# A four-layer graph network on one core: edges sorted by a scatter and gathered row by row, against edges ranked into tiles of one source and one destination group and fetched by one-hot products

## The chip, the core and the metric

The kernel runs on one core of a Trainium2 chip. The metric is the device time of one execution in microseconds (us), the median of several timed runs. Traces come from a separate, profiled execution of the same program.

## The reference

A graph of N = 12500 nodes with 64 features and E = 200000 edges (src, dst, a type out of 33, a weight) passes through four layers, each added to its input and layer-normalised. The list is sorted by dst.

```python
x = layernorm(x + L0(x))   # two hops on a hyperbolic ball
x = layernorm(x + L1(x))   # two rounds of messages and a GRU cell
x = layernorm(x + L2(x))   # two mean convolutions, 16 hidden
x = layernorm(x + L3(x))   # two mean convolutions, 128 hidden

# L0, per hop: an edge (head = src, tail = dst, relation) makes a message
res = relu(logmap(project(mobius_add(expmap(e[tail], h), expmap(rel, h))), h) + 1e-7 * ricci)
e   = l2_normalize(segment_sum(res, head) / clip(count, 1))    # h = expmap0(e[head])
# L1, per round: linear messages, summed by src, then a GRU
# L2, L3, twice each: segment_sum(x[src], dst) / degree, then two matrices
```

All of L0's maps are vectors times scalars per edge: with dot products of head, tail and relation rows, a chain of scalar operations gives three coefficients per edge, and the message is relu(c0 head + c1 tail + c2 relation). L1 needs per node the sum of x[dst] over its edges by src; L2 and L3 need the sum of x[src] by dst.

## The kernel before

P = 128 partitions. Nodes lie in NB = 98 blocks of 128. The function `fast` does the work; `general` (line 76) is a slower path that runs after it only if a flag says that the edges did not fit the fast path's tiles. Sums in f32 are kept by splitting a table into three bf16 parts (`split`, line 978), multiplying each part by an exact 0/1 matrix, and adding.

1. **Sort (lines 850-960).** VectorE (DVE) and ScalarE (ACT) count edges per source block, a scan gives each edge its slot, and GpSimd (POOL) scatters each column of 128 edges into `meta` in DRAM with one indirect DMA (line 955, 1563 of them). Each source block gets C = 18 columns of 128 edge slots: 98 x 18 = 1764 tiles.
2. **Hops (`hyper_nodes` 1040, `hyper_hop` 1243), twice.** Work goes in 42 steps of HT = 42 tiles, each cut into three of 14. For a tile: POOL gathers the tail rows by an indirect DMA (line 1273, one per tile); SyncE's (SP) queue loads the tile's source and relation indices replicated over the partitions; DVE compares them with the partition number into 0/1 matrices (1291); TensorE (PE) fetches head and relation rows by these (1299, 1303); ACT copies them out of PSUM (1305, 1306). `dots` (1311) multiplies and reduces, `edge_coefficients` (1095) is the chain of 91 small DVE operations with five ACT functions between them, `weigh` (1321) multiplies each row by its coefficient on ACT (1326), `send` (1328) adds the three rows, applies relu and sums by source with an f32 one-hot product (1334, 1337, 1338, 1350). The order on PE, DVE, ACT and POOL is written out by hand (`manual_schedule`) at the end of `hyper_hop`; elsewhere the framework orders the instructions by priority as their buffers come free.
3. **Layer end (1418-1431), then bucketing (1434-1515).** In 7 rounds of 14 source blocks `meta` is read again and each edge is ranked within its pair of source block and group of 512 destinations (NG = 25); `lane` one-hots (1491) times `v` (1470) put the local indices into 98 x 25 = 2450 tiles. Columns `slc`, `dlc` and rows `sl_rows`, `dl_rows` hold them.
4. **Passes.** `sum_to_sources` (1527, twice for L1) and `sum_to_destinations` (1579, four times: two 16 wide, two 64 wide) run over the 2450 tiles. A pass fetches with one 0/1 matrix, ACT casts the result to bf16 (1569, 1620), and a second 0/1 matrix scatters it. The 512-node side takes four matmuls, the 128-node side one: five a tile, of 192 columns (three bf16 parts of 64) or 48.
5. Dense layers (GRU, matrices) follow on blocks of 4 x 128 nodes; they are the same in both kernels.

Of the kernel before, what the change touches and what calls it, by code (L numbers as in the profile page):

```python
# [11 lines left out]
F32 = mybir.dt.float32  # L12
BF16 = mybir.dt.bfloat16
# [40 lines left out]
C = 18  # L54
BCAP = C * P
NTS = NB * C
EC = -(-E // P)
EL = E - (P - 1) * EC
SG = 4 * P
NG = -(-N // SG)  # L60
NBX = 4 * NG
IB = 14
IG = 5
HT = 42
HS_ = 14
HG = 7
TW = D + 3
RW = D + 5
HN = D + 8
SCAN = (163, 300, 550, 550)  # L70
assert sum(SCAN) == EC and IB * C % HT == 0 and HT % HS_ == 0 and HS_ % HG == 0 and NB % IB == 0 and NG % IG == 0

# [722 lines left out]
@with_exitstack  # L795
def tile_gnn_stack(ctx: ExitStack, tc: tile.TileContext, ins, out: bass.AP):
    fl = ctx.enter_context(tc.tile_pool(name="flag", bufs=1))
    flag = fl.tile([1, 1], I32, name="flag")
    fast(tc, ins, out, flag)
    full = tc.nc.values_load(flag[0:1, 0:1], min_val=0, max_val=P)  # L800
    with tc.If(full > 0):
        general(tc, ins, out)
# [3 lines left out]
def fast(ctx: ExitStack, tc: tile.TileContext, ins, out: bass.AP, flag):  # L806
# [12 lines left out]
    def iota(name, shape, pattern, base=0, mult=0, dtype=F32):  # L819
# [4 lines left out]
    iota_n = iota("iota_n", [P, P], [[1, P]])  # L824
    iota_d = iota("iota_d", [P, SG], [[1, SG]], dtype=F16)
    iota_1 = iota("iota_1", [P, P], [[1, P]], base=1, dtype=F16)
    iota_p = iota("iota_p", [P, 4], [[P, 4]], mult=1)
# [4 lines left out]
    before = const.tile([P, P], F32, name="before")  # L832
    pool.affine_select(out=before, in_=ones, compare_op=OP.is_gt, fill=0.0, base=0,
                       pattern=[[1, P]], channel_multiplier=-1)
    viol = const.tile([P, 2], F32, name="viol")

    def weights(name, shape):
        t = const.tile(shape, F32, name=f"w_{name}")
        nc.sync.dma_start(out=t, in_=ins[name])
        return t  # L840

    msg_e = const.tile([P, 2, D], F32, name="msg_e")
    nc.sync.dma_start(out=msg_e, in_=ins["msg_e"].rearrange("t k f -> k t f"))
    msg_n = const.tile([XW, 2, D], F32, name="msg_n")
    nc.sync.dma_start(out=msg_n, in_=ins["msg_n"].rearrange("t k f -> k t f"))
    gru_i = const.tile([D + 1, 2, 3 * D], F32, name="gru_i")
    nc.sync.dma_start(out=gru_i, in_=ins["gru_i"].rearrange("t k f -> k t f"))
    gru_h = const.tile([XW, 2, 3 * D], F32, name="gru_h")
    nc.sync.dma_start(out=gru_h, in_=ins["gru_h"].rearrange("t k f -> k t f"))
    s1_w = weights("s1", [XW, 32])  # L850
    s2_w = weights("s2", [33, D])
    t1_l = weights("t1_l", [D, P])
    t1_r = weights("t1_r", [XW, P])
    t2_w = weights("t2", [P, 2 * D])
    t2_b = const.tile([P, D], F32, name="t2_b")
    nc.sync.dma_start(out=t2_b, in_=ins["t2_b"].to_broadcast([P, D]))

    meta = dram.tile([P * NTS + P * EC, 4], F32, name="meta")  # L860
    meta_v = meta[: P * NTS, :].rearrange("(p v) f -> p v f", p=P)
    with ExitStack() as st:
        sp = st.enter_context(tc.tile_pool(name="sort", bufs=1))
        sw = st.enter_context(tc.tile_pool(name="sort_w", bufs=2))
        spp = st.enter_context(tc.tile_pool(name="sort_p", bufs=1, space=PSUM))

        keys = {}
        for k in ("src", "dst", "etype", "eweight"):
            t = keys[k] = sp.tile([P, EC], F32 if k == "eweight" else I32, name=f"k_{k}")
            vec.memset(t[96:P, EL:], float(P * (P - 1)) if k == "src" else 0.0)  # L870
            flat = ins[k].rearrange("p j -> (p j)")
            rows_in = flat[: (P - 1) * EC].rearrange("(p j) -> p j", j=EC)
            nc.sync.dma_start(out=t[:112, :], in_=rows_in[:112, :])
            nc.sync.dma_start(out=t[112 : P - 1, :], in_=rows_in[112:, :])
            nc.sync.dma_start(out=t[P - 1 : P, :EL], in_=flat[(P - 1) * EC :].unsqueeze(0))

        VQ = NTS // 4
        pad = sp.tile([P, VQ, 4], F32, name="pad")
        vec.memset(pad, 0.0)
        vec.memset(pad[:, :, 0], float(SG * 32))  # L880
        vec.memset(pad[:, :, 1], -1.0)
        for j in range(4):
            nc.sync.dma_start(out=meta_v[:, j * VQ : (j + 1) * VQ, :], in_=pad)

        ib = sw.tile([P, EC], I32, name="ib")
        ts(ib, keys["src"], 7, None, OP.logical_shift_right)
        kb = sp.tile([P, EC], BF16, name="kb")
        copy(kb, ib)


        QB = 42
        edge = sp.tile([P, NB + 1], F32, name="edge")
        pool.iota(edge, pattern=[[-1, NB + 1]], base=0, channel_multiplier=0, allow_small_or_imprecise_dtypes=True)
        ts(edge, edge, 0.5, None, OP.add)
        cnt = sp.tile([P, NB], F32, name="cnt")
        sgn = sp.tile([P, NB + 1], F32, name="sgn")
        for b in range(NB + 1):
            if b < QB:
                junk = sw.tile([P, EC], BF16, name="junk")
                ts(junk, kb, float(b), None, OP.is_equal, OP.add, accum_out=cnt[:, b : b + 1])  # L900
            else:
                junk = sw.tile([P, EC], BF16, name="junk_a")
                act.activation(junk, kb, AF.Sign, bias=edge[:, b : b + 1], accum_out=sgn[:, b : b + 1])
        tt(cnt[:, QB:], sgn[:, QB:NB], sgn[:, QB + 1 :], OP.subtract)
        ts(cnt[:, QB:], cnt[:, QB:], 0.5, None, OP.mult)
        pre = spp.tile([P, NB], F32, name="pre")
        pe.matmul(pre, before, cnt, start=True, stop=True)
        tot = spp.tile([P, NB], F32, name="tot")
        pe.matmul(tot, ones, cnt, start=True, stop=True)
        vec.tensor_reduce(viol[:, 0:1], tot, AX.X, OP.max)  # L910
        first = sp.tile([P, NB], F32, name="first")
        pool.iota(first, pattern=[[BCAP, NB]], base=-1, channel_multiplier=0, allow_small_or_imprecise_dtypes=True)
        tt(first, first, pre, OP.add)

        M = sp.tile([P, EC, 4], F32, name="M")
        copy(M[:, :, 0], keys["dst"])
        ib = sw.tile([P, EC], I32, name="ib")
        ts(ib, keys["src"], P - 1, None, OP.bitwise_and)
        copy(M[:, :, 1], ib)
        act.copy(M[:, :, 2], keys["etype"])  # L920
        act.copy(M[:, :, 3], keys["eweight"])

        n_max = max(SCAN)
        ones_e = sp.tile([P, n_max], BF16, name="ones_e")
        vec.memset(ones_e, 1.0)
        j0 = 0
        for n in SCAN:

            js = slice(j0, j0 + n)
            slot = sw.tile([P, n_max], F32, name="slot")[:, :n]  # L930
            vec.memset(slot, 2.0 * P * NTS)
            for b in range(NB):
                m = sw.tile([P, n_max], I16, name="m")[:, :n]
                ts(m, kb[:, js], float(b), None, OP.is_equal)
                run = sw.tile([P, n_max], F32, name="run")[:, :n]
                vec.tensor_tensor_scan(run, ones_e[:, :n], m, first[:, b : b + 1], OP.mult, OP.add)
                vec.copy_predicated(slot, m, run)
                if j0 + n < EC:
                    act.copy(first[:, b : b + 1], run[:, n - 1 : n])
            over = sw.tile([P, n_max], F32, name="over")[:, :n]  # L940
            stt(over, kb[:, js], -float(BCAP), slot, OP.mult, OP.add)
            none = sw.tile([P, n_max], I16, name="none")[:, :n]
            ts(none, over, float(BCAP), None, OP.is_ge)
            behind = sw.tile([P, n_max], I32, name="behind")[:, :n]
            pool.iota(behind, pattern=[[1, n]], base=P * NTS + j0, channel_multiplier=EC)
            si = sw.tile([P, n_max], I32, name="si")[:, :n]
            copy(si, slot)
            lane = sw.tile([P, n_max], I32, name="lane")[:, :n]
            ts(lane, si, P - 1, None, OP.bitwise_and)
            ts(si, si, 7, None, OP.logical_shift_right)  # L950
            pos = sp.tile([P, n], I32, name=f"pos{j0}")
            stt(pos, lane, float(NTS), si, OP.mult, OP.add)
            vec.copy_predicated(pos, none, behind)
            for c in range(n):
                s = pool.indirect_dma_start(  # L955
                    out=meta[:, :], out_offset=bass.IndirectOffsetOnAxis(ap=pos[:, c : c + 1], axis=0),
                    in_=M[:, j0 + c, :], in_offset=None)
# [875 lines left out]
```

## Time and profile before

| | us |
|---|---|
| timed runs, median of 3 | 16375.89 (16375.42 to 16382.63) |
| profiled execution | 19517.08 |
| its span | 19515.4 |
| sort and scatter | 0 to 2409 |
| hop 1, hop 2 | 2550 to 6905, 7075 to 11425 |
| bucketing | 11660 to 12460 |
| passes of L1 (64 wide) | the first 12480 to 13570, the second up to 15004 |
| passes of L2 (16 wide) | 15436 to 16245, 16250 to 17064 |
| passes of L3 (64 wide) | 17164 to 18300, 18400 to 19450 |

The profiled execution is 3141 us longer than the median. Busy time over the span: PE 9427.2 us (48%), weight loads 8637.0 (44%), DVE 12080.7 (62%), ACT 7308.8 (37%), POOL 5227.6 (27%). The mean granted TensorE clock is 0.694. Lines below are read so: a group gives line, engine, operation, out<-in with shape, count, then busy time, mean ns of one, and idle time before it with what ended it; a timeline row gives start, length, engine, line, count.

### The profile page before, as it was taken

To read this page: it belongs to the slowest core of one execution; us is meant where nothing else is said; L and a number is where in the kernel's file an instruction comes from. 1 tells how busy PE (TensorE), PEld (TensorE's weight loads), DVE (VectorE), ACT (ScalarE), POOL (GpSimd) and SP (SyncE) were. 2 spreads that over 40 slices of the span, in tenths; PEclk is the share of its full clock that TensorE was granted. 3 is DMA by queue.
4 is the path that set the end of the run, shared out by engine and by line. 5 is a ranking of instruction groups with operands and counts; after the bars stand their busy time and mean duration, and the time that the engine had idled before them with its cause. 6 is when DMAs were issued, how large, how long until landed. Compare 5 with 4: busy or idle time off the path is not lost. (4 is left out here: it accounts for less than half of the span.)

```text
span 19515.4 us, 307194 instructions
## 1 busy us (share of the span) xinstructions
PE 9427.2 (48%) x106965; PEld 8637.0 (44%) x106965; DVE 12080.7 (62%) x34976; ACT 7308.8 (37%) x22359; POOL 5227.6 (27%) x5108
## 2 busy tenths in 40 slices
PE   0000013333333313333233323599899888889998
PEld 0000013323232312223222222598798677789898
DVE  6800035555555545554555579997697599988788
ACT  2000024444444424444444430254354233355555
POOL 3877733444344324434433400000000000000000
PEclk9999965555555555555555555798798555589999
DMA  0000031111121131111111110121121133222122
GB/s 16 1 2 2 11 66 44 45 42 46 44 47 44 38 54 45 41 44 47 42 44 43 43 35 6 40 76 57 40 76 54 40 102 101 96 68 75 57 73 72
DMA packets 557119, 934.39 MB, mean 48 GB/s; under 512 B 313712, under 2 KB 316027, under 8 KB 555562
## 3 DMA queue, kind: packets, MB, share of 16 engines
q1 hardware_dynamic: 392650, 790.07, 12.8%
q0 software_dynamic: 162912, 124.55, 4.2%
q8 instruction: 856, 14.02, 0.3%
q14 instruction: 701, 5.74, 0.1%
HBM read 878.49 MB, written 35.70 MB: 47 GB/s over the span
## 5 line engine op out<-in xcount | busy, mean ns | idle before, releaser
L1273 POOL DMA_INDIRECT T<-tab_h,ix x3528 | 3538.0, 1003 | 5367.0 <-DVE HS L1337 3761.4
L1350 PE MATMUL ps<-msg,oh 128*128 128x66 f32 (+1 forms) x7056 | 1549.3, 410 | 3781.3 <-ACT RS L1326 1319.0
L1598 PE MATMUL ps<-gb,d 128*128 128x192 bf16 (+2 forms) x39200 | 3298.1, 232 | 20.3 <-DVE d L1596 12.3
L1350 PEld LDWEIGHTS ps<-msg,oh 128*128 128x128 f32 x7056 | 1503.7, 323 | 3786.0 <-ACT RS L1326 1498.6
L1596 DVE TENSOR_SCALAR d<-iota_d,dl 128x512 bf16<-128x512 f16 x9800 | 2928.4, 349 | 291.2 <-PE ps L1598 45.4
L1598 PEld LDWEIGHTS <-d 128*128 128x128 bf16 x39200 | 2691.9, 107 | 197.8 <-DVE d L1596 30.7
L1620 ACT CAST gb<-pg 128x384 bf16<-128x384 f32 (+2 forms) x4900 | 1692.2, 361 | 1978.1 <-PE pg L1616 1666.8
L1564 PE MATMUL pg<-xs,dt 128*128 128x192 bf16 x19600 | 2049.0, 248 | 168.3 <-DVE dt L1559 168.3
L955 POOL DMA_INDIRECT meta<-M,pos x1563 | 1685.6, 1078 | 717.1 <-issue 475.8
L1299 PE MATMUL ph<-hx,st 128*128 128x69 bf16 x10584 | 767.0, 226 | 2259.5 <-issue 1682.0
L1564 PEld LDWEIGHTS <-dt 128*128 128x128 bf16 x19600 | 1676.7, 99 | 180.2 <-issue 170.9
L1299 PEld LDWEIGHTS <-st 128*128 128x128 bf16 x10584 | 606.4, 119 | 2420.3 <-issue 2088.1
L1569 ACT CAST gb<-pg 128x384 bf16<-128x384 f32 x2450 | 1171.4, 478 | 970.2 <-PE pg L1564 852.9
L1334 DVE TENSOR_TENSOR oh<-iota_n,mt 128x1792 f32<-128x1792 f32 x252 | 508.7, 2019 | 1590.1 <-remote 1328.2
L1616 PE MATMUL pg<-xs,st 128*128 128x192 bf16 (+2 forms) x9800 | 1200.0, 231 | 305.9 <-DVE st L1612 260.8
L1559 DVE TENSOR_SCALAR dt<-row,iota_p 128x640 bf16<-128x640 f16 x3920 | 1225.3, 379 | 71.9 <-PE pg L1564 62.8
L1326 ACT ACTIVATE HS<-HS,wh 128x64 f32<-128x64 f32 x3528 | 1178.3, 334 | 1.5 <-DVE wh L1236 1.5
L1326 ACT ACTIVATE T<-T,wtr 128x64 f32<-128x64 f32 x3528 | 1177.2, 334 | 0.1
L1326 ACT ACTIVATE RS<-RS,wtr 128x64 f32<-128x64 f32 x3528 | 1177.3, 334 | 0.0
L1024 PE MATMUL tr<-ident,mt 128*126 128x128 f32 x28 | 10.2, 459 | 2316.7 <-DMA rel<-in_rel_dram 2299.6
L1352 ACT COPY sums<-ps 128x66 f32<-128x66 f32 (+1 forms) x196 | 41.7, 213 | 2721.7 <-remote 1984.1
L1024 PEld LDWEIGHTS tr<-ident,mt 128*126 128x126 f32 x28 | 5.2, 195 | 2321.7 <-issue 2299.8
(389 smaller groups left out, 15713.7 us busy)
## 6 DMA issues: line engine op xcount, KB each, us to landing
row<-sl_rows SPq DMA_DIRECT2D x700, 448.0 KB
row<-dl_rows SPq DMA_DIRECT2D x196, 800.0 KB
row_st<-s_rows SPq DMA_DIRECT2D x252, 448.0 KB
row_rt<-y_rows SPq DMA_DIRECT2D x252, 448.0 KB
T<-tab_h,ix POOLq DMA_INDIRECT x3528
meta<-M,pos POOLq DMA_INDIRECT x1563
mt<-meta SPq DMA_DIRECT2D x21, 504.0 KB
heads<-hx SPq DMA_DIRECT2D x14, 724.5 KB
```

The lines of the kernel that those rows point to most:

```text
L955: s = pool.indirect_dma_start(out=meta[:, :], out_offset=bass.IndirectOffsetOnAxis(ap=pos[:, c : c + 1], axis=0), in_=M[:, j0 + c, :], in_ ...
L1273: pool.indirect_dma_start(out=T[j][:, k, :], out_offset=None, in_=table[:, :], in_offset=bass.IndirectOffsetOnAxis(ap=edges_of(v)[1][:, v ...
L1299: pe.matmul(ph[:, k, :], hot[0][:, g0 + k, :], edges_of(v)[2][:, v // C % IB, q * RW : (q + 1) * RW], start=q == 0, stop=q == 2)
L1326: act.mul(x, x, c[:, t0 + k : t0 + k + 1])
L1350: pe.matmul(acc["ps"], oh[:, k, :], msg[:, k, :], start=c == 0, stop=c == C - 1)
L1559: ts(dt[:, q, :, :], row[:, g0 : g0 + IG, :], iota_p[:, q : q + 1], None, OP.is_equal)
L1564: pe.matmul(pg[:, len(jobs), :], dt[:, q, g - g0, :], xs[:, 4 * g + q, :], start=q == 0, stop=q == 3)
L1569: act.copy(gb, pg)
L1596: ts(d, iota_d, dl[:, k, b : b + 1], None, OP.is_equal)
L1598: pe.matmul(pss[h // 2][:, h % 2, :], d[:, h * P : (h + 1) * P], gb[:, q, :], start=b == 0 and h % 2 == 0, stop=b == NB - 1, skip_group_ch ...
L1616: pe.matmul(pg[:, len(jobs), :], s[:, b - b0, :], xs[:, b, 0:wx], start=True, stop=True)
L1620: act.copy(gb, pg)
```

## The change

1. **List.** The sort, the scatter and the bucketing go. Both node sides are now cut into NG = 49 groups of GN = 256, which gives 49 x 49 = 2401 pairs, one tile of 128 lanes for each. The list is sorted by dst, so a destination group is one stretch of it. A code 64 * (dst >> 8) + (src >> 8) and six bf16 payload columns (local src, local dst, type, weight in three parts) are written to DRAM in list order; every eighth edge is counted to estimate where each destination group begins.
2. **Windows.** For each of the 49 destination groups a window of 36 x 128 = 4608 edges is loaded. A one-hot `og` of the source group, PE products that count earlier edges of the same pair, and a max tree give each edge its rank; 36 products of `lane` and `v` place the payload in the tiles.
3. **Hops.** A step is one source group, cut into NS = 7 sub-steps of HG = 7 tiles. Tails are fetched like heads, by one-hot products on a table in SBUF (`tabx`, filled by a second `split` in `hyper_nodes`). The sum by source is done in bf16 with the message split in three. The copies into `nn` and `hc` are POOL's. `edge_coefficients` yields after each operation, so that its operations alternate with the bulk of the same sub-step; phases end at "wait".
4. **Passes.** One `sum_pass` for both directions: each side takes two matmuls a tile, four in all. The scattering matrix `s` is one comparison for seven tiles, with the tile index innermost, so that PE reads its columns 14 bytes apart. ACT casts up to 7 tiles together when they are narrow, two at 64 wide.
5. **Other.** The flag tells of a pair with more than 128 edges or an edge outside its window. The loads of the dense layers' weights move from the start to the end of the hops.

The core of the diff:

```python
# list
gd = dst >> 8;  gh = gd[:, ::8]                          # 125 x 1600, 125 x 200
for b in range(NG):
    ts(junk, gh, float(b), None, OP.is_lt, OP.add, accum_out=cnt[:, b : b + 1])
...
for b in range(NG):                                      # windows
    at = nc.sync.value_load(begin[0:1, b : b + 1], ...)
    nc.sync.dma_start(out=code, in_=l_code[ds(at, WIN)]...)
    nc.sync.dma_start(out=pay, in_=l_pay[:, ds(at, WIN)]...)
    ts(ga, code, -64.0 * b, None, OP.add)
    tt(og, iota_a, ga.unsqueeze(1).to_broadcast([P, GA, WC]), OP.is_equal)      # 52 x 36
    for c in range(WC):
        pe.matmul(pc, unit[:, WC-1-c : 2*WC-1-c], og[:, :, c], ...)
    act.copy(per, pc)
    for h in range(WC // RC):
        pe.matmul(prv[:, h], upto, og[:, :, h*RC : (h+1)*RC].rearrange("p a c -> p c a"), ...)
        for c in range(RC):
            pe.matmul(prv[:, h, c, :], later[:, h*RC + c, :], per, ...)
    tt(m, og, prv, OP.mult)
    while n > 1:                                         # 52 -> 26 -> 13 -> 7 -> 4 -> 2 -> 1
        tt(m[:, 0:k, :], m[:, 0:k, :], m[:, n-k : n, :], OP.max)
    ...
    tt(lane, iota_l, rank.unsqueeze(1).to_broadcast([P, P, WC]), OP.is_equal)
    for f in range(NPAY):
        tt(v[:, f], og[:, 0:NG, :], pay[:, f, :].unsqueeze(1).to_broadcast([P, NG, WC]), OP.mult)
    for c in range(WC):
        pe.matmul(po, lane[:, :, c], v[:, :, :, c], start=c == 0, stop=c == WC - 1)
    ...
# hops
def front(n):
    nc.sync.dma_start(out=row, in_=hop_rows[...].to_broadcast([P, HG * 3 * P]))
    ts(o0, row, iota_p[:, 0:1], None, OP.is_equal)               # HG x 3 x 128
    ts(o1, row[:, :, 0:2, :], iota_p[:, 1:2], None, OP.is_equal)
    # per tile: 6 matmuls to ph (head), 6 to pt (tail, from tabx), 3 to pr (relation)
def dots(n):
    pool.tensor_copy(nn[:, 0, s, :], T[n][:, :, 0:3])
    pool.tensor_copy(nn[:, 1, s, :], RS[n][:, :, 0:3])
    pool.tensor_copy(hc[:, s, :], HS[n][:, :, D:])
    for o, x, y in (...):                                        # three times
        tt(q, x, y, OP.mult); yield
        vec.tensor_reduce(o, q, AX.X, OP.add); yield
def part2(n):
    tt(mx[n][:, :, 2*D : 3*D], HS[n][:, :, 0:D], mx[n][:, :, D : 2*D], OP.subtract); yield
    tt(oh, iota_r, slc[:, k, s].unsqueeze(1).to_broadcast([P, GN, HG]), OP.is_equal); yield
    for t in range(HG):
        for q in range(2):
            pe.matmul(ps[k][:, q, :], oh[:, q*P : (q+1)*P, t], mx[n][:, t, :], ...)
PLAN = ((0,), (1,), (2,), (3, 4))       # phases of the coefficients in sub-steps 0 to 3
for s in range(n_all + lag_w + 5):      # lag_w = 13
    banks = front(s)
    weigh(s - lag_w)
    evacuate(s, *banks)                 # three ACT copies
    bulk = chain(part2(s-lag_w-3), add(s-lag_w-1), rest(s-lag_w-2), dots(s-2), ...)
    for _ in chain(*(phase(k) for _ in PLAN[g])):
        next(bulk, None)                # one of the chain, then one of the bulk
    for _ in bulk: pass
    part1(s - lag_w - 2); part0(s - lag_w - 1)
# passes, per group k of IG = 7, per j0 of 7 tiles
for q in range(2):
    ts(o[:, q, :, :], row[:, j0 : j0 + HG, :], iota_p[:, q : q + 1], None, OP.is_equal)
tt(s, iota_r, sc[:, k, j0 : j0 + HG].unsqueeze(1).to_broadcast([P, GN, HG]), OP.is_equal)
for j in range(j0, j0 + HG):
    for q in range(2):
        pe.matmul(pg[:, len(jobs), :], o[:, q, j - j0, :], xs[:, 2*j + q, 0:wx], ...)
    # after an ACT cast to gb, two more:
    #   pe.matmul(ps[:, h, :], s[:, h*P : (h+1)*P, j % HG], gb[:, q, :], ...)
```

`add` is two sums of the three rows, `rest` takes the first bf16 part off the relu'd message, `part0` and `part1` are ACT's casts to the first two parts. In `edge_coefficients` the five ACT functions stand where they stood: tanh ends phase 0, square root phases 1 and 2, two logarithms phase 3.

## Prediction

> **What bounds the kernel now.** I read the windows by stage first. Columns: window, length, then busy time and count for PE, PEld, DVE, ACT, POOL, granted clock, DMA share, GB/s.
>
> ```profile
> 0.00:2409.00 2409.00, 1.15 (x4) 0.93 (x4) 737.00 (x1315) 153.02 (x411) 1689.62 (x1580) 1.00 0.03 4
> 2550.00:6780.00 4230.00, 1319.56 (x13608) 1222.04 (x13608) 2186.49 (x5222) 1816.54 (x6354) 1763.91 (x1764) 0.54 0.19 45
> 11660.00:12460.00 800.00, 287.05 (x1968) 185.81 (x1968) 732.02 (x2128) 60.12 (x257) 0.00 (x0) 0.50 0.02 6
> 15436.00:16245.00 809.00, 705.19 (x12250) 594.30 (x12250) 771.73 (x2659) 272.34 (x1276) 0.00 (x0) 0.53 0.30 102
> 17164.00:18300.00 1136.00, 1079.34 (x12438) 1049.27 (x12438) 928.72 (x2689) 619.57 (x1311) 0.00 (x0) 0.97 0.22 72
> ```
>
> The sort and its scatter are POOL's (2409 us). In a hop no engine is busy over 52%. Bucketing is DVE's. A 16-wide pass is DVE's (772 of 809), a 64-wide one PE's (1079 of 1136). The waits say what holds a hop:
>
> ```profile
> POOL T L1273 <- DVE HS L1337: 3761.4, 121, 91.4
> DVE oh L1334 <- remote: 1328.2, 67, 24.4
> ```
>
> POOL's gathers and DVE wait for each other in a ring. Then rates, from groups and timeline:
>
> ```profile
> L1318 DVE TENSOR_TENSOR q<-HS,T 128x896 f32<-128x896 f32 x252 | 274.8, 1090 | 196.4 <-ACT HS L1305 140.5 <-issue 54.9
> L1479 DVE TENSOR_TENSOR inc<-inc,og x7: 3440/3441/3441, 11658.1 to 12378.5; 128x6300 f16<-128x6300 f16 x7
> L1470 DVE TENSOR_TENSOR v<-og,pay x196: 937/945/960, 11606.1 to 12356.7; 128x450 f16<-128x450 f16 x196
> L1477 PE MATMUL base<-inc,before_h x7: 781/781/781, 11650.6 to 12370.9; 128*128 128x350 f16 x7
> 6779.91 0.33 ACT L1326 ACTIVATE HS<-HS,wh 128x64 f32<-128x64 f32 x1
> 6780.15 0.33 ACT L1326 ACTIVATE T<-T,wtr 128x64 f32<-128x64 f32 x1
> 5018.22 1.43 PE L1299 MATMUL ph<-hx,st 128*128 128x69 bf16 x21
> 5019.46 1.21 PE L1303 MATMUL pr<-relx,rt 128*128 128x67 bf16 x21
> 5020.51 0.85 PE L1299 MATMUL ph<-hx,st 128*128 128x69 bf16 x21
> 5021.20 0.84 PE L1303 MATMUL pr<-relx,rt 128*128 128x67 bf16 x21
> 17331.01 0.82 PE L1598 MATMUL ps<-gb,d 128*128 128x192 bf16 x8
> 17331.67 0.33 PE L1616 MATMUL pg<-xs,st 128*128 128x192 bf16 x2
> 17331.83 0.41 PE L1598 MATMUL ps<-gb,d 128*128 128x192 bf16 x3
> ```
>
> The reader is to see: DVE takes 1.04 ns an element plus 155 in f32, half per element with 16-bit operands in rows (L1479), 1.75 ns when it reads 16-bit elements 36 bytes apart (L1470). A wide strided moving read on PE (L1477) is also slow: I put it at 1.7 ns a column, estimated as the 781 ns less the 180 that L1492's 217 ns for 50 columns leaves beside its columns at 0.8. ACT's weighing muls start 0.24 us apart though 0.33 long. PE's 21 matmuls take 1.24 us in a slow stretch (59 ns each) and 0.69 in a fast one (33). The 192-column pass issues 10 in 0.82 us: 82.5 ns each, weight loads hidden.
>
> **What the Trainium skill says.** "VectorE: DVE Perf Modes", the perf-mode tier table, gives tensor_tensor on 16-bit SBUF operands twice the f32 rate; L1479 agrees (3441 ns against 6717 for L1478 with a PSUM operand). "SBUF — State Buffer", Specifications (TRN2), has 16-byte lines and a penalty for crossing to a new one; L1470 agrees. "TensorE: Matmul & The Clock Gate", Weight-path perf modes, has 128-column 16-bit weights loaded as four parallel chunks "packed or strided"; no run here shows a strided one. "SBUF — State Buffer", Who interferes with whom: a GpSimd op that reads SBUF and a DVE op with two SBUF inputs exclude each other; the trace has no such POOL op.
>
> **Profiled against timed.** The profiled execution took 19517 us, 2 outside its span of 19515; the median is 16376. The missing 3141 I put on the gathers. Outside the two hops (2550-6905 and 7075-11425, 8705 us) lie 10810, so timed hops take 5566, 2783 each, still above DVE's busy 2186 there. PE at 82.5 ns for 192 columns and DVE at its rates have nothing to give, so it can't be spread over the passes. The changed kernel has no gathers, so I take its timed run equal to its profiled one and compare with 16376. Against 19517 the same sum is a fall of 2687, which would be the profile's doing.
>
> **Front end (steps 1, 2).** Removed: sort and scatter 2409, bucketing 800. Added: list arithmetic, 49 counts of 200 elements (0.35 us each, from L900's fixed part), some 12 ops of 1600 elements, loads and stores of the list: 100. Then 49 windows. DVE each: og 1.1, m from PSUM 2.1 (3.4 if its strided PSUM read costs as L1470), six max steps 1.9, lane 2.6, six v of 1764 at 1.07 less overlap 6.0, small ones 1.3: 15-17 us. PE each: 36 po matmuls of 294 columns read 72 bytes apart, 36 x 294 x 1.7 = 18.0; pc 36 x 52 x 1.7 = 3.2; pr 4 x 468 x 1.7 = 3.2; 36 small at 64 ns 2.3; transposes 1: 28. PE works on the next window while DVE ranks this one (two buffers of og, lane and v), so PE's 28 sets the pace; latency and single buffers of pc and pr add 2, my allowance: 30, so 1470, and 20 at the end. Unknown is the strided read at the fast clock: below, 17 us (DVE) a window, 830; above, 41 us if PE and DVE alternate (m to v, 13, beside PE's 28), 2010. The window loads (SP) and rank tables' stores lie beside 210 us of work for 7 windows; uncovered they cost about 5 us a window. Sum 1590. Only inputs with over 128 edges in a pair or outside a window run the general path as well; counted on the reference's inputs, the fullest pair has 118.
>
> **Hops (step 3).** Tiles rise from 1764 to 2401. A sub-step has 7. DVE: o0 2688 elements at L1612's rate (1792 in 680 ns) 0.84, o1 0.65, six dots ops of 448 at 0.65 (467 + 155 + 30 between dependent ones) 3.9, add 1.2, rest 0.65, third part 0.55, oh 1792 16-bit elements 1.05: 8.84, seven times 61.9. Coefficients: 91 ops, 21.0 us by the groups of L1110-L1240, 24 with 49 columns and gaps of 0.035. finish 0.6. Interleaving saves about 0.2 us for each of 34 pairs, 6.8. 79.7 us a group.
> ACT: 21 muls x 0.24 = 5.0, three evacuations 1.4, two parts 1.0, coefficients and three table loads 0.8: 8.3 a sub-step, beneath DVE's 11.4. PE: 105 matmuls at 33-59 ns 3.4-6.2, 14 of 192 columns 1.2-2.3: below too. Rows of 688 KB a sub-step are 60 GB/s, against 102 in the pass above: hidden.
> **New wait:** phases 3 and 4 share a sub-step. DVE's next op after the logarithms waits for ACT, which first evacuates what PE is still multiplying: o0/o1 1.5, PE to about 6.5, evacuation 7.1, table 8.4, two Ln 8.9; DVE arrives at 4.2. It stands 4.8 us once a group, with the rest of dots queued behind it; the next fronts wait for those. Bounds: nothing if ACT runs ahead, 7 with slow PE. A gain is excluded: phase 4 can't start before phase 3 in the same queue.
> 84.5 x 49 = 4140, ramps 60: 4200, both 8400. POOL's three or four small copies a sub-step can each hold DVE up for some 0.2 us, where reduces don't cover them: I take 0.36 us x 686 = 250 (0 to 600). Sum 8650, against 5566 timed: 3084 more. The part of oh that each scattering matmul loads as weights is read 14 bytes apart; even at 220 ns (see the passes) 14 of them bring PE to 3.4-6.2 + 3.1, still below DVE: nothing.
>
> **Passes (step 4).** 2401 tiles x 4 matmuls at 82.5 = 792 (before 12250, 1011), loop ends 98: 890, four times 3560. DVE makes 7 tiles in 1.75 us (two of 896 at 0.37, one of 1792 at 1.01), 250 ns a tile against PE's 330: hidden. 16-wide: DVE's 250 x 2401 = 600 and 100: 700, twice 1400. Sum 4960; before 5999, a gain of 1039. Unknown: s is read 14 bytes apart as weights. Below: four parallel chunks, 32 x 1.7 = 55 ns, beneath the 82 of a matmul, nothing. Above: 128 x 1.7 = 220. I take nothing.
>
> **Rest (step 5 and what stays).** Hop preparation 335 (before 311; the table's split adds 2 x 22, the row transposes go), first layer end 240 (235 and 5 for the 11 weight loads now queued on SP after the hops), everything else 1056, unchanged.
>
> Sum: 1590 + 335 + 8650 + 240 + 4960 + 1056 = **16831**.
>
> **Rivals.**
> (a) Forecast, slower: gathers gone, but 36% more tiles on DVE. Own range 16350 to 17500.
> (b) Faster: PE's strided moving read isn't the window's limit. At 17 us a window 640 go: 16190. It decides below about 20 us a window. For: L1477 ran at clock 0.50. Against: DVE pays the same 1.7 at its own clock.
> (c) Faster: ACT ahead of DVE and POOL out of its way, -720: 16110. For: ACT has 3 us of slack; against: the Ln follow the evacuation in ACT's queue.
> (d) Slower still: strided weights load as one stream. Two tiles of a pass then take 4 x 82.5 + 4 x 220 = 1210 ns for 660, 1550 a pass, and 1310 for a 16-wide one: +3860, 20690; at half that load +750, 17580. For: every strided read here is slow; against: the four chunks.
> (e) The general path runs too: excluded by the count.
>
> **How the numbers follow.** (a) 0.46, (b) 0.16, (c) 0.15, (d) 0.23. Faster is (b), (c) less 0.02; same takes those 0.02 and 0.03 of (a) near 16376; the rest is slower. 0.2% is about what a measurement of this kernel tells from no change. (b) and (c) together give 15470; (d) reaches past 19000 only at its full price. Range 15500 to 19000.
>
> **What would show it.** DVE over 90% busy in hops of about 4200 us with lines of L1318's kind at 620 ns; a DVE stand of some 5 us before the first op on lg, 49 times a hop; POOL's copies beside; windows about 30 us apart with PE's po matmuls over 500 ns; 64-wide passes of 890 with 82.5 ns a matmul. Wrong if hop DVE is under 80% busy, if windows take 20 us, or if s weights take over 100 ns apart.

## The result, and the profile after

| | median, us | runs |
|---|---|---|
| before | 16379.09 (16375.42 to 16382.63) | 4 |
| after | 16957.59 (16954.58 to 16963.65) | 4 |

After over before is 1.0354 (95% interval 1.0336 to 1.0372): slower by 579 us. The profiled execution of the changed kernel took 16959.64 us (span 16957.8, clock 0.79), 2 us from its median.

On another chip the kernel before took 19132 us (19090.71 to 19143.40, three runs) instead of 16379, and the 19517 of its profile is of that kind; three variants of the changed kernel took 16442 to 16676 there, so there the change would be a gain. The changed kernel itself was not run on that chip.

The windows by stage, in the columns of the prediction: list and windows, first hop, first 64-wide pass, first 16-wide pass.

```profile
0.00:1640.00 1640.00, 1490.05 (x5639) 555.00 (x5639) 710.52 (x1201) 63.00 (x202) 42.73 (x110) 1.00 0.09 10
1759.00:6027.00 4268.00, 2196.72 (x40817) 2075.40 (x40817) 3886.84 (x9018) 2857.55 (x9358) 521.85 (x1759) 0.76 0.17 59
...
10554.00:11520.00 966.00, 882.86 (x9604) 840.42 (x9604) 710.64 (x1051) 591.17 (x1253) 0.00 (x0) 0.95 0.23 83
13245.00:13989.00 744.00, 495.77 (x9604) 468.71 (x9604) 662.06 (x1058) 165.35 (x392) 0.00 (x0) 0.53 0.30 107
```

The sort and bucketing (3209 us in the profile of before) have become 1640 us of lists and windows, and these are PE's (1490 busy). A hop is DVE's, busy 91% of 4268 us. A 64-wide pass is still PE's.

The groups that stand where L1318, L1477 and L1479 stood:

```profile
L954 PE MATMUL po<-v,lane 128*128 128x294 bf16 x1764 | 985.9, 736 | 20.4 <-DVE lane L948 20.4
...
L1336 DVE TENSOR_REDUCE hd<-q 128x7 f32<-128x448 f32 x1372 | 846.8, 617 | 27.2
L1376 DVE TENSOR_TENSOR oh<-iota_r,slc 128x1792 bf16<-128x1792 f16 x686 | 835.7, 1218 | 0.0
L1293 DVE TENSOR_SCALAR o<-row,iota_p 128x1792 bf16<-128x1792 f16 x686 | 781.8, 1140 | 0.0
```

Operations of 448 elements take 617 ns, as forecast. The two one-hots are longer than forecast: `oh` 1218 for 1050, `o1` (L1293) 1140 for 650. In place of the ring of POOL and DVE there is one wait, in the list of DVE's waits over the first hop, and in the timeline of one group:

```profile
DVE z L1252 <- ACT lg L1250: 238.4, 48, 5.6
```

```profile
3998.98 1.28 ACT L1249 ACT_TABLE_LOAD   x1
4000.28 0.24 ACT L1249 ACTIVATE lg<-n 128x49 f32<-128x49 f32 x1
4000.43 0.23 ACT L1250 ACTIVATE lg<-n 128x49 f32<-128x49 f32 x1
4000.69 0.21 DVE L1252 TENSOR_TENSOR z<-lg 128x49 f32<-128x49 f32 x1 [4.43 <-ACT lg L1250]
```

DVE stands 5.0 us on average (238.4 / 48) once a group: ACT reaches the table load and the two logarithms late.

The whole against the prediction's sum (stage borders by the first and last instruction of each):

| term | predicted | measured |
|---|---|---|
| list and windows | 1590 | 1640 |
| preparation of the hops | 335 | 119 + 136 = 255 |
| two hops | 8650 | 4268 + 4269 = 8537 |
| end of the first layer | 240 | 122 |
| four 64-wide passes | 3560 | 966 + 962 + 962 + 960 = 3850 |
| two 16-wide passes | 1400 | 744 + 735 = 1479 |
| the rest (what remains of the span) | 1056 | 1075 |
| sum | 16831 | 16958 |

### The profile page after: what moved, and what is told of

The parts are those of the page before. It is cut to its first block, busy times and chain, and to the rows that moved or that the text cites. A ratio compares the mean times of both kernels' runs of the same rounds, so it can differ in the third digit from the quotient of the medians.

```text
span 16957.8 us, 370716 instructions
## 1 busy us (share of the span) xinstructions
PE 11219.9 (66%) x148137; PEld 9596.6 (57%) x148137; DVE 13305.5 (78%) x26837; ACT 8790.9 (52%) x25310; POOL 812.7 (5%) x2903
## 5 line engine op out<-in xcount | busy, mean ns | idle before, releaser
L1300 PE MATMUL ph<-hx,o 128*128 128x69 bf16 x28812 | 1728.8, 236 | 4277.8 <-DVE o L1291 3496.8
L1300 PEld LDWEIGHTS <-o 128*128 128x128 bf16 x28812 | 1520.4, 124 | 4506.5 <-DVE o L1291 3627.3
L1571 PE MATMUL pg<-xs,o 128*128 128x192 bf16 (+2 forms) x28812 | 2956.1, 237 | 637.0 <-DVE o L1564 636.0
L1543 PE MATMUL ps<-gb,s 128*128 128x192 bf16 (+2 forms) x28812 | 2993.1, 238 | 357.6 <-ACT gb L1551 336.5
L1543 PEld LDWEIGHTS <-s 128*128 128x128 bf16 x28812 | 2600.8, 137 | 564.1 <-issue 378.2
L1566 DVE TENSOR_TENSOR s<-iota_r,sc 128x1792 bf16<-128x1792 f16 x2058 | 2507.4, 1223 | 447.9 <-PE ps L1543 422.6
L1571 PEld LDWEIGHTS <-o 128*128 128x128 bf16 x28812 | 2171.0, 105 | 657.0 <-issue 641.8
L1564 DVE TENSOR_SCALAR o<-row,iota_p 128x896 bf16<-128x896 f16 x4116 | 1661.9, 448 | 404.8 <-PE pg L1571 259.8
L1305 PE MATMUL pt<-tabx,o 128*128 128x67 bf16 x28812 | 1422.1, 222 | 0.0
L1305 PEld LDWEIGHTS <-o 128*128 128x128 bf16 x28812 | 1363.3, 118 | 0.0
L1382 PE MATMUL ps<-mx,oh 128*128 128x196 bf16 (+1 forms) x9604 | 960.2, 253 | 139.9 <-DVE oh L1376 133.7
L954 PE MATMUL po<-v,lane 128*128 128x294 bf16 x1764 | 985.9, 736 | 20.4 <-DVE lane L948 20.4
L1336 DVE TENSOR_REDUCE hd<-q 128x7 f32<-128x448 f32 x1372 | 846.8, 617 | 27.2
L1376 DVE TENSOR_TENSOR oh<-iota_r,slc 128x1792 bf16<-128x1792 f16 x686 | 835.7, 1218 | 0.0
L1293 DVE TENSOR_SCALAR o<-row,iota_p 128x1792 bf16<-128x1792 f16 x686 | 781.8, 1140 | 0.0
```

What stands on the lines that cost most here:

```text
L954: pe.matmul(po, lane[:, :, c], v[:, :, :, c], start=c == 0, stop=c == WC - 1)
L1300: pe.matmul(ph[:, t, :], o[:, t, 0, :], head[k][:, q, i * RW : (i + 1) * RW], start=q + i == 0, stop=q + i == 3)
L1305: pe.matmul(pt[:, t, :], o[:, t, 1, :], tabx[:, 2 * (g * HG + t) + q, i * TW : (i + 1) * TW], start=q + i == 0, stop=q + i == 3)
L1336: vec.tensor_reduce(o, q, AX.X, OP.add)
L1376: tt(oh, iota_r, slc[:, k, s].unsqueeze(1).to_broadcast([P, GN, HG]), OP.is_equal)
L1382: pe.matmul(ps[k][:, q, :], oh[:, q * P : (q + 1) * P, t], mx[n][:, t, :], start=g + t + q == 0, stop=g * HG + t == HT - 1, skip_group_che ...
```

## The experiments

**Where the 3141 us between profile and median lie.** The prediction put them on the gathers and on the taking of a profile. First the kernel before with one hop:

```diff
-    for hop in range(2):
+    for hop in range(1):
         table, heads = hyper_nodes(res)
```

> The kernel before with its second hop (and that hop's preparation) left out, so what follows works on the first hop's result. In the profile of before this part is 4520 us (170 of preparation, 4350 of hop). The theory of the prediction says that the 3141 us between the profiled 19517 and the timed 16376 are the gathers', half in each hop: the timed run should fall by 2783 + 170 = 2953 to about 13423, the profiled one by 4520 to about 14997, and the difference between the two halve to some 1570. Rival: the difference is spread over the whole execution; then the timed run falls by 4520 x 16376/19517 = 3793 to 12583. Second rival: it lies outside the hops; then the timed run falls by 4520 to 11856 and the difference stays at 3141.

Measured: 14735.77 (two runs, the profiled one 14758.68), on the chip where the whole kernel took 19131.86. The hop is worth 4396 us in timed runs too, and profiled and timed runs differ by 46 us. All three expectations failed, because the base itself was 19132: it is not the profile that lengthens the hops but something that differs between chips, or between the occasions on which they were used. This chip was met on one occasion, the one that gave 16397 and 16404 us for the kernel before on two; the two causes are not separated.

> The changed kernel as it is, once more, on whichever chip comes. In the first runs of this study the kernel before took 19132 us where it had taken 16376 earlier. Theory: the difference lies between chips, in the gathers alone, and the changed kernel, bound by PE in the windows and the 64-wide passes and by VectorE in the hops, takes 16958 within 0.3% on any of them; its ratio to the kernel before then goes from 1.035 to 0.886, whichever chip it is. Rival: the chip as a whole is slower or faster; then the changed kernel moves with the kernel before and the ratio stays near 1.035.

The chip that came had the kernel before at 16396.90. The changed kernel took 16975.05 (16965.13 to 16983.02), ratio 1.0355 (1.0338 to 1.0372): the result again. The question of the other chip wasn't put by this run.

```diff
-                for k in range(HS_):
-                    v = j * HS_ + k
-                    pool.indirect_dma_start(out=T[j][:, k, :], ..., in_=table[:, :], ...)
+                edges_of(j * HS_)
+                at = j * HS_ % NB
+                nc.sync.dma_start(out=T[j], in_=rows(table)[:, at : at + HS_, :])
```

> The kernel before with GpSimd's gather of T (28 indirect DMAs a batch of two tiles of 14) replaced by plain loads of as many contiguous rows on SyncE's queue, so that T holds other rows than the edges ask for; all else is kept. Theory: the difference of 2750 us between executions of the kernel before is the gathers'; without them the hops are bound by the order of VectorE, PE and ScalarE, at 2250 us (VectorE's 2186 busy) to 2783 each on any chip: 15300 to 16400. Rival: it lies in something else of the hops (loads of rows, SyncE); then this kernel takes over 17500 on a chip where the kernel before takes 19100.

Measured: 16371.36, beside 16396.90 with gathers: 0.9986 (0.9979 to 0.9993). Here the gathers are hidden to within 26 us; they are not what holds the hop, and the ring of POOL and DVE that the prediction read from the waits is no bound here. From the first one-hot to the last sum its hops took 2873 and 2803 us.

> The kernel before as it is, for its trace on the chip that comes. On one chip it took 16397, and with plain loads in place of the gathers 16371 with hops of 2790 us; on another 19132. Theory: where it takes 16.4 ms, its hops are 2800 us each with the gathers hidden; where it takes over 19, they are 4200 to 4350 and every other stage is as long as on the first. Rival: the other stages differ too, by over 1%.

Measured: 16405.86, and so a profile of the kernel before that agrees with its median. From the first one-hot to the last sum its hops take 2902 and 2838 us, against 4385 and 4433 in the long profile: 3078 of the 3111 us between the two spans. What follows the hops differs by 2 us in 8010. The sort, whose scatters are indirect DMAs of POOL too, issues the last of them 54 us earlier (at 2352 for 2406, 2%), so the rival holds for that stage. Windows that lie within the two hops, then PE's waits for nothing that the profile shows ("issue"), over the same 2700 us of the first hop, in the long profile of before and in this one:

```profile
2550.00:5340.00 2790.00, 1174.74 (x13789) 1159.92 (x13789) 2250.24 (x5380) 1880.46 (x6574) 1855.99 (x1731) 0.58 0.29 66
5500.00:8300.00 2800.00, 1194.69 (x13944) 1181.04 (x13944) 2260.19 (x5241) 1856.58 (x6394) 1889.81 (x1764) 0.58 0.32 70
```

```profile
PE ph L1299 <- issue: 416.9, 290, 4.0
PE ps L1350 <- issue: 253.2, 122, 15.2
...
PE pr L1303 <- issue: 122.5, 107, 2.6
```

```profile
PE pr L1303 <- issue: 1.2, 2, 0.9
```

DVE is busy 81% of such a window. The prediction inferred 2783 us a hop, from borders drawn too early; with the borders above its subtraction gives (8818 - 3141) / 2 = 2839, and the measured mean is 2870. In the long profile PE stands 793 us in such gaps (1.4 to 2.1 us on average in the first two rows), in the short one 1 us. Over the whole first hop they come to 1245 us, and that hop is 1483 us longer. On the chip of the one-hop run they were 769 us in the same stretch. That the gathers provoke these gaps is likely and not shown: plain loads were not run on a chip that has them.

The next three experiments ran once each, on the chip where the kernel before took 19132, and are set beside the 16958 of the result. The stages that they leave alone have the same length there as in the result's profile: windows come 31.5 us apart in two of them as in the changed kernel (the third changes them), and PE's part of the first 64-wide pass is 953 to 954 us in all three, for 955.

**Windows: is PE's strided moving read the limit (rival b)?**

```diff
+            vc = wp.tile([P, WC, NPAY, NG], BF16, name="vc")
+            for f in range(NPAY):
+                act.copy(vc[:, :, f, :], v[:, f].rearrange("p a c -> p c a"))
-                pe.matmul(po, lane[:, :, c], v[:, :, :, c], ...)
+                pe.matmul(po, lane[:, :, c], vc[:, c], ...)
```

> The changed kernel with one step more in each of the 49 windows: ScalarE, idle there, copies v into a tile ordered by column, and PE reads that one contiguously in its 36 matmuls of 294 columns. Theory: the strided moving read is what makes such a matmul take 545 ns (735 as shown, overlapped); it falls to about 150, PE's share of a window falls from 30 to some 15 us, and ScalarE (six copies of 1764 elements, 9 us at 0.83 ns an element, 18.5 if a strided read costs it 1.75) or VectorE (13.3) sets a pace of 16 to 20: 49 x 11.5 to 15 less, 16220 to 16400. Rival: the strided weights (lane, 72 bytes apart) or the accumulation hold these matmuls; then they stay at about 545 ns and the time does not fall.

Measured: 16442.51, 515 less. PE's rows of one window, after (28 of its 36 matmuls are shown) and in this kernel, and the groups of this kernel's windows:

```profile
816.85 15.69 PE L954 MATMUL po<-v,lane 128*128 128x294 bf16 x28
```

```profile
820.77 5.88 PE L957 MATMUL po<-vc,lane 128*128 128x294 bf16 x36
```

```profile
L954 ACT COPY vc<-v 128x1764 bf16<-128x1764 bf16 x288 | 972.7, 3490 | 0.0
L957 PE MATMUL po<-vc,lane 128*128 128x294 bf16 x1764 | 325.1, 361 | 0.0
```

A matmul of 294 columns takes 0.56 us with the columns 72 bytes apart (15.69 / 28) and 0.16 with neighbouring ones (5.88 / 36; from window to window 0.16 to 0.20, at a mean granted clock of 0.67 where the strided ones had 1.00); the weights (`lane`) are strided in both. Windows fall from 31.5 to 20.6 us apart, and ACT's six copies of 3.49 us now set the pace. Rival (b) is out: the strided read was PE's limit, and the forecast price of 1.7 ns a column was 1.9.

**Hops: the stand ahead of the logarithms (rival c).**

```diff
-PLAN = ((0,), (1,), (2,), (3, 4))
+PLAN = ((0,), (1,), (2,), (3,), (4,))
```

> The changed kernel with phases 3 and 4 of the coefficients in two sub-steps instead of one (one more sub-step of delay before weighing, one more buffer each of HS, T and RS, one less of a small tile of the finish). Theory: VectorE's stand of 5.0 us ahead of the first operation on lg, 98 times, is the order of the two phases and goes whole: 490 us less, 16470, with the wait gone from VectorE's list. Rival: ScalarE is behind anyhow because PE gets its one-hots last in each sub-step; the stand then moves to another operation and the time stays within 100 us of 16958.

Measured: 16498.45, 459 less, and of the 238 us in DVE's waits over the first hop there remain

```profile
DVE z L1252 <- ACT lg L1250: 5.3, 2, 3.4
```

All but 31 of the 490 us came away, and the largest wait in their place is 18 us, for ACT's `mx`: it was the order of two phases.

**Hops: the second one-hot.**

```diff
-                row = wp.tile([P, HG, 3, P], F16, name="row")
+                row = wp.tile([P, 3, HG, P], F16, name="row")
-                ts(o1, row[:, :, 0:2, :], iota_p[:, 1:2], None, OP.is_equal)
+                ts(o1, row[:, 0:2, :, :], iota_p[:, 1:2], None, OP.is_equal)
```

(and `hop_rows`, `hr`, `o0`, `o1` in the same order of dimensions.)

> The changed kernel with the three fields of a row table kept field by field within a sub-step's seven tiles, in DRAM and SBUF, so that the second comparison (o1) reads one contiguous run of 1792 elements instead of seven runs of 256 with gaps; nothing else differs. Theory: its 1140 ns against the 680 of the same size in one run is the gaps' doing; it falls to about 680, and since VectorE is the bound of the hops 686 x 0.46 = 315 us go: 16640. Rival one: the width of what is written sets it, it stays at 1140 and nothing changes. Rival two: it falls but the hop is held by the ring of VectorE, PE and ScalarE rather than by VectorE's work, and less than half of the 315 comes through.

Measured: 16676.23, 281 less, with the instances of the operation (min/median/max):

```profile
L1293 DVE TENSOR_SCALAR o<-row,iota_p x686: 673/679/690, 1761.0 to 10023.7; 128x1792 bf16<-128x1792 f16 x172
```

1140 ns come to 679 by the order of the fields alone, and 89% of it comes through: a hop is DVE's own time. Whether the gaps count, or that seven rows are read where one run is written, isn't separated.

**Hops: POOL's copies.**

```diff
+                for _ in range(2):
                     pool.tensor_copy(nn[:, 0, s, :], T[n][:, :, 0:3])
                     pool.tensor_copy(nn[:, 1, s, :], RS[n][:, :, 0:3])
                     pool.tensor_copy(hc[:, s, :], HS[n][:, :, D:])
```

> The changed kernel with GpSimd's three small copies of each sub-step made twice (same values): 686 x 3 copies more. The prediction put 250 us on these and a fourth one holding VectorE up. Theory now: none of it happens, since VectorE's operations have the same 0.60 to 0.63 us with and without a copy beside them; the time stays within 40 us of 16965. Rival (the prediction's): each copy holds VectorE up by a share of its 0.26 to 0.36 us, and the same 190 to 250 us come once more: 17150 to 17220.

Measured: 17004.23 (one run), beside 16975.05 on the same chip: 29 us for 2058 copies more, where 190 to 250 were to come, and the four runs of the changed kernel there lie up to 18 us apart. The prediction's term was nearly nothing (its fourth copy, in the first hop alone, was not doubled).

The trace of the changed kernel shows that it is POOL that waits. A copy that starts beside one of DVE's multiplications (L1334, two operands from SBUF) takes 0.42 us on average (406 copies), one that starts beside a reduction (L1336) 0.21 (736). The multiplications take 0.62 us either way: 624 ns where a copy was under way at their start, 620 elsewhere. The two forms of o1 differ in this too: beside the one of 1140 ns a copy takes 0.20 us (180 copies), beside the one of 679 ns, in the experiment before, 0.62 (21).

**Passes: strided weights (rival d).**

```diff
-                                pe.matmul(ps[:, h, :], s[:, h * P : (h + 1) * P, j % HG], gb[:, q, :],
+                                at = (j % HG) * GN + h * P
+                                pe.matmul(ps[:, h, :], s.rearrange("p c t -> p (c t)")[:, at : at + P], gb[:, q, :],
```

> The changed kernel with the passes' scattering matmuls loading their weights from 128 neighbouring elements of s instead of every seventh (14 bytes apart), so that the passes sum the wrong edges; the work is the same. In the 64-wide passes eight matmuls take 0.72 us, 90 ns each, and the prediction had 82.5. Theory: the four with strided weights pay for it: 7.5 ns x 9604 x 4 passes = 290 less, 16670, and their weight loads shown at 130 ns come to the 98 of o's. Rival: PE pays for changing between two accumulations or waits for ScalarE's copies; then 16958 stays within 50 us.

Measured: 16882.43 (one run), 93 less than on the same chip. The 64-wide passes stayed (963, 959, 960 and 958 us, for 963, 961, 958 and 960 on that chip), the 16-wide ones fell from 743 and 734 to 702 and 688. Twelve scattering matmuls of a 16-wide pass, after and with this edit:

```profile
13501.49 0.80 PE L1543 MATMUL ps<-gb,s 128*128 128x49 bf16 x12 [0.59 <-ACT gb L1551]
```

```profile
13501.99 0.66 PE L1544 MATMUL ps<-gb,s 128*128 128x49 bf16 x12 [0.59 <-ACT gb L1552]
```

So my theory of the 64-wide passes fell, and the next one was a ring over ACT.

```diff
-                    while len(pend) > (0 if last else 1):
+                    while len(pend) > (0 if last else 2 if w == D else 1):
```

> The changed kernel with one edit in the 64-wide passes: the scattering matmuls run two pairs of tiles behind the gathering ones instead of one, with the same buffers. With neighbouring weights these passes stayed at 960 us, so the weights are not what makes 16 matmuls take 1.44 us instead of 1.32. Theory: it is a ring. PE's scatter of a pair waits for ScalarE's copy of that pair (0.48 us after PE's last gathering matmul of it), with only 8 matmuls, 0.66 us, in between; one pair more of distance hides it, a matmul comes to 82.5 ns, and 72 us go in each of four passes: 290 in all, about 16680. Rival: PE itself pays at every second change between its two accumulations, or VectorE delivers o and s too late; then the passes stay within 15 us of 960 and the time within 60 of 16970.

Measured: 16688.57 (two runs), 286 less than on the same chip. PE's order in a 64-wide pass, after and with this edit (starts; four matmuls a row):

```profile
11199.89 0.49 PE L1571 MATMUL pg<-xs,o 128*128 128x192 bf16 x4
11200.24 0.49 PE L1543 MATMUL ps<-gb,s 128*128 128x192 bf16 x4
11200.56 0.49 PE L1571 MATMUL pg<-xs,o 128*128 128x192 bf16 x4
11201.00 0.49 PE L1543 MATMUL ps<-gb,s 128*128 128x192 bf16 x4
11201.33 0.49 PE L1571 MATMUL pg<-xs,o 128*128 128x192 bf16 x4
11201.68 0.49 PE L1543 MATMUL ps<-gb,s 128*128 128x192 bf16 x4
```

```profile
11200.12 0.49 PE L1571 MATMUL pg<-xs,o 128*128 128x192 bf16 x4
11200.45 0.49 PE L1543 MATMUL ps<-gb,s 128*128 128x192 bf16 x4
11200.78 0.49 PE L1571 MATMUL pg<-xs,o 128*128 128x192 bf16 x4
11201.11 0.49 PE L1543 MATMUL ps<-gb,s 128*128 128x192 bf16 x4
```

With a distance of one pair the scatters start 0.76 and 0.68 us apart in turn, with two always 0.66: 82.5 ns a matmul. The passes took 888, 885, 886 and 885. The list of waits shows nothing of this ring, since a matmul is drawn 0.25 us long and one slot of 0.08 us disappears behind its modelled end; the starts show it.

**Together.**

> Phases 3 and 4 in two sub-steps, rows kept field by field, and v turned for PE, all three, with one of the six turning copies on VectorE instead of ScalarE. Alone they gave 459, 281 and 515 us (16958 less 16498, 16676, 16442). Theory: they lie in different places and add up, and the moved copy shortens a window from ScalarE's 21 to some 18 us, 150 more: 16958 - 1255 - 150 = 15550. Rival: with VectorE's stand and o1 gone, ScalarE (8.3 us of a sub-step by the prediction) or the ring over PE becomes the hop's bound and a third of the 740 in the hops is lost: 15800.

Measured: 15746.87, ratio 0.9607 (0.9591 to 0.9623): 1228 less on its chip. The three add up, and give some 50 us more (1255 less the 80 below would be 1175); the moved copy does not help. Groups of its windows:

```profile
L954 ACT COPY vc<-v 128x1764 bf16<-128x1764 bf16 x204 | 689.6, 3441 | 103.1 <-DVE v L951 102.8 <-ACT per L925 0.4
...
L954 DVE COPY vc<-v 128x1764 bf16<-128x1764 bf16 x41 | 74.5, 1818 | 0.0
```

The copy takes DVE 1.8 us, but ACT now waits for `v`, which DVE has ready later, and windows come 22.3 us apart instead of 20.6: 80 us lost where 150 were hoped for.

> Phases 3 and 4 in two sub-steps, rows kept field by field, v turned with all six copies on ScalarE, and the scatter of the 64-wide passes two pairs behind. With five copies on ScalarE and one on VectorE the first three together gave 15747, and a window took 22.3 us against 20.6 with all six on ScalarE: 80 us back. Theory: 15747 - 80 - 290 = 15380. Rival: the longer distance gains nothing: 15670.

Measured: 15376.59 (15374.56 to 15380.78), ratio to before 0.9375 (0.9362 to 0.9388). This version beats both kernels: the one before by 6.3% and, against 16975 on the same chip, the changed one by 9.4%.

## Why the prediction was right, point by point

- **Forecast.** 16830 for 16957.59, on the right side and by the mechanism of case (a): lists and windows take 1569 us less than sort and bucketing did, the passes 670 less, and the hops lose more. From first instruction to last the hops went from 2902 + 2838 = 5740 to 8537, +2797; the forecast's +3084 started from 5566. That the sum came within 0.8% is in part luck: misses of +50, +369 and +19 stand against -80, -113 and -118. There are 36% more tiles, and DVE spends 1.62 us on each (3887 / 2401) for 1.30 (2294 / 1764). A tile's one-hots cost it 0.47 us (911, 1140 and 1218 ns for seven tiles) for 0.25 (739, 682 and 2019 ns for fourteen), and the split of the message into bf16 parts, which the kernel before does without, adds 0.17 (L1360 and L1372, 619 and 601 ns for seven).
- **The frame.** That the 3141 us belong to the hops held (3078 of 3111 by the traces). That they are the profile's doing, or the gathers' waiting, did not: timed runs on another chip have them, and where they are absent plain loads save 26 us. Most of them are gaps in PE's issue. "Against 19517 the same sum is a fall of 2687, which would be the profile's doing" was wrong in its last clause. On that other chip the same 16831 would have been a gain: the forecast's sign rests on the 16376 that it was compared with, which is not the time of every chip.
- **Windows.** 31.5 us for 30, PE's: it is busy 30.4 of them (1490 / 49) for the forecast 28, and its po term was 20.1 for 18.0 (0.56 us for 0.50). The 2 us allowed for latency covered prices that were too low.
- **Hops.** From one stand to the next 85.8 us for 84.5, ramps 62 for 60. Inside, errors cancelled: o1 and oh cost 0.49 and 0.17 us more, 4.6 a group. A sub-step without coefficients took 9.09 us from o0 to o0 (4005.99 to 4015.08) for 8.84, since an operation that doesn't depend on the one before starts some 0.08 us ahead of its end, which I had allowed for the coefficients alone. The stand was 5.0 for 4.8. POOL's 250 us were the term that failed: 29 by experiment. The Trainium skill, "SBUF — State Buffer", Who interferes with whom, has a GpSimd read and a DVE op with two SBUF inputs exclude each other; the trace agrees, with POOL as the one that waits (0.42 us a copy for 0.21), and POOL's time was not on the path.
- **Passes.** The largest miss, +369. The step "2401 tiles x 4 matmuls at 82.5 = 792" took a pace measured in a kernel with five matmuls a tile, where ten lie between a pair's fetch and its scatter; with four a tile there are eight, and ACT's 0.48 us and the two handovers no longer fit: 90 ns. With one pair more the forecast 890 is met (885 to 888). In the 16-wide passes "DVE 250 ns a tile" was 267 (three operations in 1.87 us, 13499.70 to 13501.57) and not the bound: seven tiles take 2.06 us, in which PE waits 0.59 for ACT's cast each time. That this is the same ring is read from the trace; a longer distance was not tried there. Strided weights are 41 to 46 us of each pass.
- **Strided weights.** Taken at nothing. Behind 192 columns that was right (the 64-wide passes kept their length); behind 48 or 49 columns they cost 0.14 us in twelve matmuls. The pattern itself is one that the Trainium skill, "TensorE: Matmul & The Clock Gate", Weight-path perf modes, names for the fast load ("packed or strided"), and rival (d)'s full price of 220 ns appears nowhere here.
- **Preparation and layer end.** 80 and 118 too high. My borders cut the hops of before too early: the last store of the first left at 6937, of the second at 11506, and I had cut at 6905 and 11425, so 32 and 81 us of hop were counted as preparation and layer end.

## What to carry to other kernels

Ask of a pace measured in one kernel what distance it needs: taking one matmul of five away brought a hidden copy of ACT onto the path. A one-hot that replaces a gather is paid for on the engine that makes it, so compare DVE's time per tile before and after, tiles counted. Before a gap between a profile and timed runs is explained, run the unchanged kernel once more on another chip.

## What the runs showed of the hardware

- A moving operand of 294 bf16 columns 72 bytes apart takes PE 0.56 us, one of neighbouring columns 0.16 to 0.20. The same turning read costs ACT 1.98 ns an element (3490 / 1764) and DVE 1.03 (1818 / 1764).
- A one-hot comparison of 1792 elements takes DVE 679 ns in one run, 1140 when it reads seven runs of 256 with gaps and writes without. In the first form it holds POOL's copies up (0.62 us a copy), in the second it doesn't (0.20).
- Beside DVE's multiplications of two operands from SBUF a small copy of POOL's takes 0.42 us for 0.21; DVE loses 4 ns.
- 128 columns of bf16 weights 14 bytes apart cost nothing behind matmuls of 192 columns (960 us a pass either way) and 0.14 us in twelve behind matmuls of 49.
- The kernel before took 16.4 ms on one chip and 19.1 on another, with 3078 of 3111 us of the difference in its hops, most of them gaps in PE's issue, and 54 in its sort; the stages after its hops differ by 2 us. The windows and passes of the changed kernel had the same lengths on both.
